# Cross-attention with LayerNorm: a new order of VectorE's prologue, the first query weights on ScalarE's DMA queue, and eight warm-up products

## The chip, the cores and the metric

The kernel runs on one core of one Trainium2 chip. The metric is the device time in microseconds (us) of one execution; a kernel's time is the median of its runs.

## The reference, cut to what matters

Queries `x` (4 batches, 2048 rows, 512 wide) attend to a context of 77 rows for each batch, with 16 heads of 32; a mask marks the context rows that are left out. The result goes through an output projection, is added to `x`, and is normalised by row:

```python
qs = (q @ wq).reshape(Bq, Lq, H, HD).transpose(0, 2, 1, 3)
ks_ = (k @ wk).reshape(Bq, Lk, H, HD).transpose(0, 2, 1, 3)
vs = (v @ wv).reshape(Bq, Lk, H, HD).transpose(0, 2, 1, 3)
scores = jnp.einsum('bhqd,bhkd->bhqk', qs, ks_) / jnp.sqrt(jnp.float32(HD))
scores = jnp.where(mask[:, None, :, :], -jnp.inf, scores)
attn_w = jax.nn.softmax(scores, axis=-1)
attn = jnp.einsum('bhqk,bhkd->bhqd', attn_w, vs)
out = attn @ wo + q
# LayerNorm over the row, times gamma, plus beta
```

All of it is float32.

## The kernel before

The 8192 rows are 64 tiles of 128 (`t`), 32 blocks of two tiles (`b`) and 16 groups of four tiles (`g`). Projections are exact to float32 by splitting: an operand is rounded to a high part (`wqh`, `x0h`, `woh`, `wvh`, `ctx_h`), the rest is a low part (`wql`, `x0l`, ...), and three products (high-high, high-low, low-high) are summed in PSUM. `split` makes the high part on ScalarE and the low part on VectorE.

Nothing is scheduled by a planner: `manual_schedule` is on, so every engine runs its instructions in the order in which the Python code issues them, and an engine that waits for one instruction holds all that stand behind it. Each DMA queue (SyncE's, ScalarE's, GpSimd's) is in order too. PSUM is a ring of eight banks handed out by `bank`.

The work around the change:

- **Prologue** (lines 558 to 631). VectorE clears the tile `warm`, and ten bf16 products on it (`WARM`) keep TensorE busy while the first loads come. SyncE issues the loads: half of `xT0`, `wq` by quarters, the context `ctx_f`, `wk` by quarters, the mask, the other half. For each quarter `c`, `x0` and `wq` are split, and the products of the first query half (`pq_0_m`, m = 0 to 3) are issued; then come the keys (`pk`), the copies out of PSUM, the mask bias of the first tile (`mask_bias`), the value-weight loads (`load_wv`) and `keys_evac`.
- **Main loop**, steps u = 0, 2, 4, ... each for tiles u and u+1. For a tile: `scores` (64 small products into four banks), `maxima` (sixteen VectorE instructions, one per head, which add the mask bias `mb`, write the scores to `pbuf` and reduce their maximum), `exps` (sixteen on ScalarE, with row sums), `recip` (VectorE), `normalise` (GpSimd), `transp` (VectorE's 32x32 transposes of `pbuf` into the block's tile `B`). When both tiles of a block are transposed, `regroup` issues twelve SBUF-to-SBUF DMAs from `B` into `PT` on SyncE's queue. Two steps later `av` multiplies `PT` with the values `vsb` on TensorE (line 397), and `o_proj`, `residual`, `moments`, `scale`, `affine` and `store` follow.
- There are three `pbuf` (tile t uses t mod 3), and the tag `B` has two buffers, which `ctx_f` and `ctx_h` held first.
- **Between them in the first steps**: query products for later groups (`q_visit`) with their copies (`q_evac`, VectorE); the value products (`values`, one for each of batches 0 to 2) with `values_evac` (VectorE); `split_wv` (VectorE, four subtractions); `split_wo` (GpSimd); `mask_nan`, which prepares a column that `moments` reads later; the casts and low parts of the next groups of `x` (`cast_xT` on ScalarE, `split_xT` on GpSimd, line 163).
- In step 2 SyncE's queue holds the load of half a group (`load_xT`, line 154), whose buffer `split_xT` on GpSimd must first have read, and behind it the regroup of block 0.
- From tile 54 on a list written out by hand, `ORDER`, sets the order.

VectorE's order in the first steps of the kernel before:

- step 0: maxima of tile 0 with a query copy, mask bias of the other 15 tiles, `split_wv`, query copy, `recip(0)`, maxima of tile 1, `transp(0)`, `mask_nan`, `recip(1)`;
- step 2: maxima of tile 2 with query copies, `transp(1)`, `values_evac(0)`, query copies, `recip(2)`, maxima of tile 3, `values_evac(1)` and `(2)`, `recip(3)`;
- step 4: maxima of tile 4, `transp(2)`, `transp(3)`, query copies, `recip(4)`, maxima of tile 5.

Of the kernel before, what the change touches and what calls it, by code (L numbers as in the profile page):

```python
# [17 lines left out]
P = 128  # L18
# [13 lines left out]
GRP = 2 * BLK  # L32
MASKED = -3.0e38
EPS = 1.0e-5
WARM = 10
NPB = 3
KSCALE = 1.0 / HD**0.5
LATE = 48
# [29 lines left out]
def xattn_layernorm(  # L68
# [68 lines left out]
    def wview(w, c):  # L137
        return w[c * P : (c + 1) * P, :]

    def split(hi, lo, src):  # L140
        nc.scalar.copy(hi, src)
        nc.vector.tensor_tensor(lo, src, hi.bitcast(F32), ALU.subtract)
# [9 lines left out]
    def load_xT(g, c):  # L152
        fx[g, c] = sb.tile([P, 2, GRP], F32, tag="xtf", name=f"xtf_{g}_{c}")
        nc.sync.dma_start(fx[g, c], xT[g, :, c : c + 2])
# [50 lines left out]
    def keys_evac(pks, m):  # L205
        for i, eng in ((m, nc.scalar), (m + 1, nc.vector)):
            pk = pks[i][:, : NB * (NK + 1)].rearrange("p (b k) -> p b k", b=NB)[:, :, :NK]
            for dst, src in ((kct[:, i, :, TAIL_K:], pk), (kct[:, i, :, :TAIL_K], pk[:, :, NK - TAIL_K :])):
                if eng is nc.scalar:
                    eng.activation(dst, src, AF.Copy, scale=KSCALE)  # L210
                else:
                    eng.tensor_scalar(dst, src, KSCALE, None, ALU.mult)
# [27 lines left out]
    def values_evac(r):  # L240
        pv = vd.pop(r)
        for b, p0, k0, n in ((r, 0, 0, NK2), (NB - 1, NK2, 32 * r, 32)):
            src, dst = (a.rearrange("p (q a d) -> p q a d", a=2, d=HD) for a in (pv[p0 : p0 + n], vsb[k0 : k0 + n, b]))
            rows_of = vm[k0 : k0 + n, :, 0][:, None, :, None].to_broadcast((n, NP, 2, HD))
            nc.vector.tensor_tensor(dst, src, rows_of, ALU.mult)
# [9 lines left out]
    def split_wv():  # L255
        for c in range(NC_D):
            nc.vector.tensor_tensor(wvl[c], stage_b[:, 0, c], wvh[c].bitcast(F32), ALU.subtract)
# [19 lines left out]
    def mask_bias(b, ts=slice(0, TPB)):  # L277
        mb, nz, m8 = bat[b]
        nc.vector.tensor_scalar(mb[:, ts, TAIL_K:], m8[:, ts], MASKED, None, ALU.mult)
        nc.vector.tensor_scalar(mb[:, ts, :TAIL_K], m8[:, ts, NK - TAIL_K :], MASKED, None, ALU.mult)  # L280
# [26 lines left out]
    def maxima(t, lo, hi):  # L307
        pb = pbuf[t % NPB]
        mb = bat[t // TPB][0]
        nm = nmax[t]  # L310
        for h in HEADS[lo:hi]:
            g, j = divmod(h, GH)
            nc.vector.tensor_tensor_reduce(  # L313
                pb[:, h // 2, (h % 2) * NK : (h % 2 + 1) * NK],
                scs[t][j][:, g * NK : (g + 1) * NK],
                mb[:, t % TPB, keys_of(h)],
                -1.0,
                3.0e38,
                ALU.add,
                ALU.min,  # L320
                accum_out=nm[:, h : h + 1],
            )
# [36 lines left out]
    def transp(t):  # L359
        b, tt = divmod(t, 2)  # L360
        if b not in bts:
            bts[b] = sb.tile([P, 5, 2 * NP * 32], F32, tag="B", name=f"B_{b}")
        if b < NBLK - 1:
            bt = bts[b].rearrange("p c (q t r) -> p c q t r", q=NP, t=2)[:, :, :, tt, :]
        else:
            bt = bts[b].rearrange("p c (t q r) -> p c q t r", q=NP, t=2)[:, :, :, tt, :]
        nc.vector.transpose(  # L367
            bt.rearrange("p c q r -> p q c r"),
            pbuf[t % NPB].rearrange("p q (c r) -> p q c r", c=5),
        )  # L370
# [184 lines left out]
        nc.vector.scalar_tensor_tensor(od[t], od[t], mvs[t, 1][:, 2:3], rows.get(1, bet), ALU.mult, ALU.add)  # L555


    nc.vector.memset(warm, 0.0)
    nc.gpsimd.memset(mhalf, -0.5)
    nc.gpsimd.memset(mneg, -1.0)  # L560
    for pb in pbuf:
        nc.gpsimd.memset(pb[:, :, 2 * NK :], 0.0)
    pw = bank("pw")
    for i in range(WARM):
        nc.tensor.matmul(pw, warm[:, :P], warm, start=True, stop=True)

    for c in range(0, NC_D, 2):
        fx[0, c] = sb.tile([P, 2, GRP], F32, tag="xtf", name=f"xtf_0_{c}")
# [3 lines left out]
    f0 = {c: fx[0, c].rearrange("p c r -> p (c r)").rearrange("p (h c r) -> p h c r", h=2, c=2) for c in (0, 2)}  # L572
    for c in range(0, NC_D, 2):
        nc.sync.dma_start(f0[c][:, 0], xT0[0, :, c : c + 2])
        nc.sync.dma_start(stage_a[:, 0, c], wview(wq, c))
        nc.sync.dma_start(stage_a[:, 0, c + 1], wview(wq, c + 1))
    for c in range(0, NC_D, 2):
        nc.sync.dma_start(ctx_f[:, c : c + 2], ctxT[:, c : c + 2])
    for c in range(NC_D):
        nc.sync.dma_start(stage_a[:, 1, c], wview(wk, c))  # L580
    load_mask(0)
    for c in range(0, NC_D, 2):
# [1 line left out]
    value_rows()  # L584
    pq0 = [bank(f"pq_0_{m}") for m in range(NG)]
    for c in range(NC_D):
        split(x0h[:, c], x0l[:, c], f0[c // 2 * 2][:, 0, c % 2])
        split(wqh[:, c], wql[:, c], stage_a[:, 0, c])
        for m in range(NG):
            for n, (w, r) in enumerate(((wqh, x0h), (wqh, x0l), (wql, x0h))):  # L590
                nc.tensor.matmul(
                    pq0[m][:, :BLK],
                    w[:, c, m * P : (m + 1) * P],
                    r[:, c, :],
                    start=(c == 0 and n == 0),
                    stop=(c == NC_D - 1 and n == 2),
                )
# [11 lines left out]
        split(*(a[:, c : c + 2, BLK:] for a in gx[0]), f0[c][:, 1])  # L609
    deal_last()  # L610
    q_visit(0, 0)
    mask_bias(0, slice(0, 1))
    gate(stage_a[:, 1, NC_D - 1, D - 1 :])
    load_wv()
    for m in range(0, NG, 2):
        keys_evac(pks, m)
    for c in range(0, NC_D, 2):
        fx[1, c] = stage_a[:, 0, c : c + 2]
        nc.sync.dma_start(fx[1, c], xT[1, :, c : c + 2])
# [8 lines left out]
    def visits(u):  # L628
        return early[u] if u in early else [divmod(u + 5, 4)] * (u + 5 < 4 * NGRP)

    def pieces(u):
        return casts.get(u) or [((u + 8) // 4, u % 4)] * (u + 8 < 4 * NGRP)

    evac = [(0, 0)]
    for u in range(0, 2 * CUT, 2):
        n = u // 2
        m, k = divmod(u, TPB)

        for q in pieces(u + 2):
            if u >= 4:  # L640
                load_xT(*q)
        for t in (u - 4, u - 3):
            if t >= 0:
                load_x(t)
        scores(u)
        maxima(u, 0, H // 2)
        for q in evac:
            q_evac(*q)
        maxima(u, H // 2, H)
        for q in pieces(u):  # L650
            cast_xT(*q)
        exps(u, 0, H)
        for q in pieces(u):
            split_xT(*q)
        if u == 0:
            mask_bias(0, slice(1, TPB))
            split_wv()
        if u >= 6:
            o_proj(u - 6)
        for v in {2: (0,)}.get(u, ()):  # L660
            values(v)
        for q in visits(u):
            q_visit(*q)
        if u >= 6:
            residual(u - 6)
            moments(u - 6)
        if u == 4:
            transp(2)
        if u == 2:
            load_xT(*pieces(4)[0])  # L670
        if u:
            transp(u - 1)
            regroup(n - 1)
        for v in list(vd):
            values_evac(v)
        if u >= 8:
            scale(u - 8)
            scale(u - 7)
        if u >= 8:
            affine(u - 8)  # L680
        for q in visits(u):
            q_evac(*q)
        if u == 0:
            load_wo()
            nc.gpsimd.memset(ident, 0.0)
            nc.gpsimd.affine_select(ident, ident, [[-1, P]], ALU.not_equal, 1.0, base=0, channel_multiplier=1)
        if k == TPB - 6 and m + 1 < NB:
            load_mask(m + 1)
        if k == TPB - 4 and m + 1 < NB:
            mask_bias(m + 1)  # L690
        if k == TPB - 2 and m + 1 < NB:
            mask_nan(m + 1)

        recip(u)
        if u >= 4:
            av(n - 2)
            av_hi(n - 2, 0)
            av_hi(n - 2, 1)
        scores(u + 1)
        maxima(u + 1, 0, H // 4)  # L700
        if u >= 4:
            av_lo(n - 2, 0)
        maxima(u + 1, H // 4, H // 2)
        if u >= 4:
            av_lo(n - 2, 1)
        maxima(u + 1, H // 2, H)
        normalise(u)
        for c in {0: (0, 1), 2: (2, 3)}.get(u, ()):
            split_wo(c)
        if u >= 8:  # L710
            affine(u - 7)
        exps(u + 1, 0, H // 4)
        exps(u + 1, H // 4, H)
        if u >= 5:
            o_proj(u - 5)
        if u >= 5:
            residual(u - 5)
        if u != 2:
            transp(u)
        for v in {2: (1, 2)}.get(u, ()):  # L720
            values(v)
            values_evac(v)
        evac = visits(u + 1)
        for q in evac:
            q_visit(*q)
        if u >= 5:
            moments(u - 5)
        if u == 0:
            mask_nan(0)
        recip(u + 1)  # L730
        normalise(u + 1)
        if u >= 8:
            store(u - 8)
            store(u - 7)
# [90 lines left out]
```

## Time and profile before

| what | us |
|---|---|
| median of three runs | 518.78 |
| lowest and highest of them | 516.29, 519.95 |
| time of the profiled execution | 517.11 |
| its span, first to last instruction | 515.3 |
| TensorE (PE) busy | 504.5 (98%) |
| VectorE (DVE) busy | 473.8 (92%) |
| ScalarE (ACT) busy | 470.3 (91%) |
| GpSimd (POOL) busy | 418.1 (81%) |

The mean granted clock of TensorE in the profiled execution is 0.996. In the profile's rows L313 is the line that an instruction comes from; `out<-in` are the program's tiles; x12 counts the instructions of a row; square brackets give the idle time of the engine just before the row, and what ended it. In timelines the first two columns are the start and the length in us. Matmuls are pipelined: the pace is told by the distance of their starts, not by their lengths. In a row of windows come the stretch, its length, the busy time of PE, PEld, DVE, ACT and POOL with the number of instructions in brackets, the granted clock, the DMA share and GB/s. SPq is SyncE's DMA queue, DVEq VectorE's queue of waits.

### The profile page before, as it was taken

What the parts mean: (1) busy time and instruction counts of PE and PEld (TensorE: products, weight loads), DVE (VectorE), ACT (ScalarE), POOL (GpSimd) and SP (SyncE); (2) the same over time, 40 slices, a digit from 0 to 9 for tenths busy, and PEclk for the clock granted to TensorE, in tenths of its full rate; (3) what the DMA queues carried; (4) which work ended last, traced back from release to release, by engine and by line L of the source; (5) the groups of instructions that cost most, each with busy time, mean ns of one, the idle gap of its engine ahead of it and who ended that gap; (6) DMA issues with size and microseconds to landing.
All of it is one profiled execution on the core that took longest, in us unless ns stands there. A gap on an engine that the chain in (4) does not pass through costs nothing.

```text
span 515.3 us, 20436 instructions
## 1 busy us (share of the span) xinstructions
PE 504.5 (98%) x6838; PEld 385.7 (75%) x6838; DVE 473.8 (92%) x2572; ACT 470.3 (91%) x2241; POOL 418.1 (81%) x375
## 2 busy tenths in 40 slices
PE   9999989999999999999999999999999999999994
PEld 6987767777777777777777777777777877777672
DVE  5699998899999888989999898889999989999996
ACT  6789999999899999999899999999899999999841
POOL 0658549889799988888889989889889988857996
PEclk9999999999999999999999999999999999999998
DMA  8946678787778878788778878869878887776665
GB/s 304 402 146 161 175 201 206 205 233 207 202 186 229 222 217 226 211 215 223 182 208 235 232 199 213 227 178 240 216 201 220 212 217 232 203 200 176 170 215 209
DMA packets 58936, 110.24 MB, mean 214 GB/s; under 512 B 9392, under 2 KB 11312, under 8 KB 58832
## 3 DMA queue, kind: packets, MB, share of 16 engines
q1 hardware_dynamic: 56144, 103.62, 72.6%
q0 software_dynamic: 2128, 4.85, 3.4%
q8 instruction: 55, 0.90, 0.8%
q10 hardware_dynamic: 560, 0.46, 0.3%
q14 instruction: 49, 0.40, 0.3%
HBM read 41.79 MB, written 16.78 MB: 114 GB/s over the span
## 4 chain that ended last, share of the span: by engine, by line
PE 74%; DVE 8%; POOL 5%; DMA 4%; SPq 3%; ACT 3%; issue 2%; DVEq 0%; POOLq 0%; ACTq 0%
PE po L463 30%; PE pq L170 26%; PE pa L397 9%; PE sc L299 9%; ACT pbuf L327 2%; SPq L379 2%; DVE B L367 2%; DMA PT<-B 2%; DVE pbuf L313 2%; DMA stage_b<-wo 1%; DMA stage_a<-wk 1%; POOL mvt L529 1%; POOL o_end L542 1%; DVE AL L432 1%; POOL o_end L493 1%
## 5 line engine op out<-in xcount | busy, mean ns | idle before, releaser
L327 ACT ACTIVATE pbuf<-pbuf,nm 128x77 f32<-128x77 f32 x1024 | 352.4, 349 | 17.3 <-DVE nm L313 15.8
L327 ACT ACTIVATION_READ_ACCUMULATOR pbuf<-pbuf,nm 128x1 f32 x1024 | 194.0, 189 | 0.0
L313 DVE CUSTOM_DVE_ANT_0 pbuf<-sc,mb 128x77 f32<-128x77 f32 x1024 | 170.5, 230 | 22.3 <-PE sc L299 22.2
L343 POOL TENSOR_TENSOR pbuf<-pbuf,ri 128x1232 f32<-128x1232 f32 x63 | 142.2, 2258 | 23.5 <-DVE ri L338 19.4
L170 PE MATMUL pq<-xth,wqh 128*128 128x512 f32 (+1 forms) x256 | 98.8, 386 | 0.0
L170 PE MATMUL pq<-xtl,wqh 128*128 128x512 f32 (+1 forms) x256 | 97.9, 382 | 0.0
L170 PE MATMUL pq<-xth,wql 128*128 128x512 f32 (+1 forms) x256 | 97.9, 382 | 0.0
L367 DVE STREAM_TRANSPOSE B<-pbuf 128x1280 f32<-128x1280 f32 x64 | 95.5, 1493 | 2.2 <-DMA PT<-B 1.7
L463 PE MATMUL po<-woh,AH 128*128 128x512 f32 x232 | 96.8, 417 | 0.0
L463 PE MATMUL po<-wol,AH 128*128 128x512 f32 x232 | 90.7, 391 | 0.0
L463 PE MATMUL po<-woh,AL 128*128 128x512 f32 x232 | 88.8, 391 | 0.0
L313 DVE DVE_READ_ACCUMULATOR2_ANT nm<- 128x1 f32 x1024 | 83.9, 82 | 0.0
L493 POOL TENSOR_TENSOR o<-o,gam 128x512 f32<-128x512 f32 x50 | 65.6, 1312 | 14.4 <-ACT o L489 14.3
L299 PEld LDWEIGHTS sc<-kct,q 32*64 32x64 f32 x4096 | 51.4, 130 | 24.2 <-issue 23.5
L494 POOL TENSOR_TENSOR o<-o,bet 128x512 f32<-128x512 f32 x50 | 64.5, 1289 | 3.9
L163 POOL TENSOR_TENSOR xtl<-xtf,xth 128x1024 fp32r<-128x1024 f32 x28 | 67.0, 2394 | 0.0
L299 PE MATMUL sc<-kct,q 32*64 32x77 f32 x4096 | 61.5, 237 | 0.3 <-DVE nm L313 0.3
L397 PE MATMUL pa<-PT,vsb 96*32 96x256 f32 x960 | 58.0, 382 | 1.9 <-DVE st L471 1.3
L170 PEld LDWEIGHTS pq<-xth,wqh 128*128 128x128 f32 x256 | 48.1, 188 | 9.8
L170 PEld LDWEIGHTS pq<-xth,wql 128*128 128x128 f32 x256 | 48.1, 188 | 9.4
L170 PEld LDWEIGHTS pq<-xtl,wqh 128*128 128x128 f32 x256 | 48.1, 188 | 9.1
L463 PEld LDWEIGHTS po<-woh,AH 128*128 128x128 f32 x232 | 43.5, 187 | 12.5 <-issue 0.7
(139 smaller groups left out, 700.5 us busy)
## 6 DMA issues: line engine op xcount, KB each, us to landing
PT<-B SPq DMA_DIRECT2D x352, 128.0 KB
xtf<-xT SPq DMA_DIRECT2D x28, 512.0 KB
o<-x SPq DMA_DIRECT2D x56, 256.0 KB
out<-o SPq DMA_DIRECT2D x56, 256.0 KB
PT<-B POOLq DMA_DIRECT2D x20, 128.0 KB, 4.0
o_end<-x SPq DMA_DIRECT2D x8, 256.0 KB
out<-o_end SPq DMA_DIRECT2D x8, 256.0 KB
xtf<-xT SPq DMA_DIRECT2D x4, 256.0 KB
```

The lines of the kernel that those rows point to most:

```text
L163: nc.gpsimd.tensor_tensor(l, fx.pop((g, c)), h.bitcast(F32), ALU.subtract)
L170: nc.tensor.matmul(pq, w[:, c, m * P : (m + 1) * P], r[:, c, rs], start=(n == 0), stop=(n == 11))
L299: nc.tensor.matmul(sc[j][half : half + P // 2, g * NK : (g + 1) * NK], qs[q, g, r0 : r0 + P // 2], kct[q, g, t // TPB, keys_of(j)], start= ...
L313: nc.vector.tensor_tensor_reduce(pb[:, h // 2, (h % 2) * NK : (h % 2 + 1) * NK], scs[t][j][:, g * NK : (g + 1) * NK], mb[:, t % TPB, keys_ ...
L327: nc.scalar.activation(pb[:, h // 2, (h % 2) * NK : (h % 2 + 1) * NK], pb[:, h // 2, (h % 2) * NK : (h % 2 + 1) * NK], AF.Exp, bias=nmax[t ...
L343: nc.gpsimd.tensor_tensor(pv, pv, rv.to_broadcast((P, NP, 2, NK)), ALU.mult)
L367: nc.vector.transpose(bt.rearrange("p c q r -> p q c r"), pbuf[t % NPB].rearrange("p q (c r) -> p q c r", c=5),)
L379: queue.dma_start(pts[b][32 * c : 32 * c + 32, i, :, cols], src)
L397: nc.tensor.matmul(pas[b, g // 2][HD * j : HD * (j + 1), (g % 2) * BLK : (g % 2 + 1) * BLK], vsb[:, 2 * b // TPB, HD * h : HD * (h + 1)], ...
L463: nc.tensor.matmul(pos[t], a[:, c, rs], w[:, c, :], start=(first and n == 0), stop=(n == 11))
L493: nc.gpsimd.tensor_tensor(o, o, gam, ALU.mult)
L494: nc.gpsimd.tensor_tensor(o, o, bet, ALU.add)
```

## The change

VectorE's order in the first steps becomes:

- prologue: VectorE itself copies the high part of `wq`'s first quarter; the mask bias of eight tiles instead of one; `mask_nan` right after the keys' copies;
- step 0: maxima of tile 0 with a query copy, mask bias of the other eight tiles, query copy, maxima of tile 1, `split_wv`, `recip(0)`;
- step 2: half of tile 2's maxima, `recip(1)`, query copies, the other half, `transp(0)`, `values_evac(0)`, `transp(1)`, `recip(2)`, maxima of tile 3, query copies, `values_evac(1)`, `recip(3)`, `transp(2)`;
- step 4: maxima of tile 4, `transp(3)`, `values_evac(2)`, query copies, `recip(4)`, maxima of tile 5.

GpSimd clears the warm-up tile (a quarter of the old width, read four times by each product), and there are eight products. The first quarter of `wq` is issued on ScalarE's queue; half of the context is issued behind the first two quarters of `wk`. The first query products are ordered by operand pair, then by `m`. GpSimd's order of the large operations, TensorE's order from the keys on, and everything from step 6 on stay.

```diff
-WARM = 10
+WARM = 8
@@
-    nc.vector.memset(warm, 0.0)
+    nc.gpsimd.memset(ident[:, : P // 2], 0.0)
@@
-        nc.tensor.matmul(pw, warm[:, :P], warm, start=True, stop=True)
+        nc.tensor.matmul(pw, warm[:, :P], warm[:, None, :P].to_broadcast((P, 4, P)), start=True, stop=True)
@@
-        nc.sync.dma_start(stage_a[:, 0, c], wview(wq, c))
+        (nc.sync if c else nc.scalar).dma_start(stage_a[:, 0, c], wview(wq, c))
         nc.sync.dma_start(stage_a[:, 0, c + 1], wview(wq, c + 1))
-    for c in range(0, NC_D, 2):
-        nc.sync.dma_start(ctx_f[:, c : c + 2], ctxT[:, c : c + 2])
     for c in range(NC_D):
+        if c % 2 == 0:
+            nc.sync.dma_start(ctx_f[:, c : c + 2], ctxT[:, c : c + 2])
         nc.sync.dma_start(stage_a[:, 1, c], wview(wk, c))
@@
     for c in range(NC_D):
+        if c == 0:
+            nc.vector.tensor_copy(wqh[:, 0], stage_a[:, 0, 0])
         split(x0h[:, c], x0l[:, c], f0[c // 2 * 2][:, 0, c % 2])
-        split(wqh[:, c], wql[:, c], stage_a[:, 0, c])
-        for m in range(NG):
-            for n, (w, r) in enumerate(((wqh, x0h), (wqh, x0l), (wql, x0h))):
+        if c == 0:
+            nc.vector.tensor_tensor(wql[:, 0], stage_a[:, 0, 0], wqh[:, 0].bitcast(F32), ALU.subtract)
+        else:
+            split(wqh[:, c], wql[:, c], stage_a[:, 0, c])
+        for n, (w, r) in enumerate(((wqh, x0h), (wqh, x0l), (wql, x0h))):
+            for m in range(NG):
@@
-    mask_bias(0, slice(0, 1))
+    mask_bias(0, slice(0, TPB // 2))
@@
         keys_evac(pks, m)
+    mask_nan(0)
@@ main loop, first half of a step
         maxima(u, 0, H // 2)
+        if u == 2:
+            recip(1)
+            normalise(1)
@@
         if u == 0:
-            mask_bias(0, slice(1, TPB))
-            split_wv()
+            mask_bias(0, slice(TPB // 2, TPB))
@@
-        if u == 4:
-            transp(2)
         if u == 2:
             load_xT(*pieces(4)[0])
+        if u == 2:
+            transp(0)
+            values_evac(0)
         if u:
             transp(u - 1)
             regroup(n - 1)
-        for v in list(vd):
-            values_evac(v)
+        if u == 4:
+            values_evac(2)
@@
-        for q in visits(u):
-            q_evac(*q)
+        if u != 2:
+            for q in visits(u):
+                q_evac(*q)
@@ second half
-        recip(u)
+        if u:
+            recip(u)
@@
         maxima(u + 1, H // 2, H)
+        if u == 0:
+            split_wv()
+            recip(0)
+        if u == 2:
+            for q in visits(u):
+                q_evac(*q)
         normalise(u)
@@
-        if u != 2:
+        if u >= 4:
             transp(u)
-        for v in {2: (1, 2)}.get(u, ()):
-            values(v)
-            values_evac(v)
+        if u == 2:
+            values(1)
+            values_evac(1)
+            values(2)
@@
-        if u == 0:
-            mask_nan(0)
-        recip(u + 1)
-        normalise(u + 1)
+        if u:
+            recip(u + 1)
+            normalise(u + 1)
+        if u == 2:
+            transp(2)
```

## The prediction

> **What bounds the kernel now.** I read the chain of waits on the page first, then the same chain in order of time, then each engine's timeline over the first 70 us, since the change touches nothing that runs later.
>
> ```profile
> PE 74%; DVE 8%; POOL 5%; DMA 4%; SPq 3%; ACT 3%; issue 2%; DVEq 0%; POOLq 0%; ACTq 0%
> ```
> TensorE sets the end. In order of time (start, length, what):
>
> ```profile
> 49.88 2.69 DMA PT<-B
> ...
> 68.22 1.93 PE pa L397 x32
> 70.15 0.88 PE sc L299 x54
> ...
> 434.29 0.89 PE sc L299 x54
> 435.18 0.22 DVE pbuf L313
> ```
> From 68.22 to 435.18 us every piece of the chain is TensorE; what follows hangs on the scores at 434.29. So whatever moves the `av` of block 1 at 68.22 moves the end one for one. Before 68.22 the chain runs through the regroup transfers, and TensorE's timeline shows where they hold it:
>
> ```profile
> 41.44 0.95 PE L299 MATMUL sc<-kct,q 32*64 32x77 f32 x64
> ...
> 57.32 0.50 PE L170 MATMUL pq<-xth,wqh 128*128 128x512 f32 x1
> ...
> 60.28 0.95 PE L299 MATMUL sc<-kct,q 32*64 32x77 f32 x64
> ...
> 66.53 0.39 PE L170 MATMUL pq<-xth,wql 128*128 128x512 f32 x1
> 68.22 1.93 PE L397 MATMUL pa<-PT,vsb 96*32 96x256 f32 x32 [1.30 <-DVE st L471]
> ```
> The last query matmul starts at 66.53 and would be followed after 0.25 us (twelve from 57.32 to 60.28), so TensorE is at `av` by 66.78 and loses 1.44 there. VectorE is named as the releaser, but the program makes this matmul wait for the twelve transfers of block 1's regroup. SyncE's timeline shows their issue:
>
> ```profile
> 41.19 0.33 SPq L154 DMA_DIRECT2D xtf<-xT  x1
> 41.62 8.86 SPq L379 DMA_DIRECT2D PT<-B  x12
> ...
> 56.17 9.22 SPq L379 DMA_DIRECT2D PT<-B  x12
> ```
> Block 0's last transfer lands by the chain at 52.57 (49.88 + 2.69). Block 1's issues end at 65.39; with the same 2.69 they land at 68.1. So 68.22 is fixed by when the second transpose of block 1 ends.
>
> **The change, part by part.** The part that decides is the transpose of tile 2 (`transp(2)`). It moves from the middle of step 4, behind all of tile 4's maxima, to the end of step 2, ahead of them. In both programs it waits for all twelve transfers of block 0's regroup, because block 1's `B` takes the buffer that these transfers read. VectorE works in order, so all that stands behind it waits too. Before, on VectorE:
>
> ```profile
> 46.71 2.81 DVE L245 TENSOR_TENSOR vsb<-pv,small 96x512 f32<-96x512 f32 x4
> 50.14 0.25 DVE L338 RECIPROCAL ri<-sum 128x16 f32<-128x16 f32 x1 [0.62 <-ACT pbuf L327]
> ...
> 53.23 2.90 DVE L367 STREAM_TRANSPOSE B<-pbuf 128x1280 f32<-128x1280 f32 x2 [0.19 <-issue]
> 56.06 1.25 DVE L187 COPY q<-pq 128x512 f32<-128x512 f32 x2
> ```
> and, in the view of line 367, the waits of VectorE's queue (least, median and longest in ns, first and last start):
>
> ```profile
> L367 DVEq EVENT_SEMAPHORE  x8: 49/50/749, 52.1 to 74.4; - x8
> ```
> The first of those waits began at 52.1; if it is the one of 749 ns, the transfers were in by 52.85, just when tile 4's maxima ended. The old order hid the wait behind these maxima. The new one has no such cover. Tile 3's maxima began at 44.2 (46.71 less 2.53, the price of sixteen worked out below) and its last reciprocal at 50.14; they now begin at 41.9 or 42 (41.44, less a start gain of 0.4, plus 0.95), so the reciprocal comes at about 47.8 and `transp(2)` is next. VectorE idles some 5 us.
>
> When do those transfers land now? SyncE's load at 41.19 stands ahead of them and waits for GpSimd:
>
> ```profile
> 30.54 2.26 POOL L343 TENSOR_TENSOR pbuf<-pbuf,ri 128x1232 f32<-128x1232 f32 x1 [4.41 <-DVE ri L338]
> 32.76 2.55 POOL L267 TENSOR_TENSOR wol<-stage_b,woh 128x512 fp32r<-128x512 f32 x2
> 36.54 2.26 POOL L343 TENSOR_TENSOR pbuf<-pbuf,ri 128x1232 f32<-128x1232 f32 x1 [1.24 <-DVE ri L338]
> 38.77 4.74 POOL L163 TENSOR_TENSOR xtl<-xtf,xth 128x1024 fp32r<-128x1024 f32 x2
> ```
> GpSimd's order stays; the first step starts when tile 0's reciprocal is done. That one is put behind tile 1's maxima and the split of the value weights. The rows that price this:
>
> ```profile
> 18.01 0.62 DVE L212 TENSOR_SCALAR kct<-pk 128x308 f32<-128x308 f32 x2 [0.95 <-PE pk L196]
> ...
> 22.59 0.24 DVE L313 CUSTOM_DVE_ANT_0 pbuf<-sc,mb 128x77 f32<-128x77 f32 x1 [3.07 <-PE sc L299]
> ...
> 25.72 1.35 DVE L279 TENSOR_SCALAR mb<-m 128x1155 bf16<-128x1155 uint8 x1
> ...
> 27.21 1.28 DVE L257 TENSOR_TENSOR wvlAH<-stage_b,wvh 128x512 fp32r<-128x512 f32 x2
> ...
> 29.61 0.68 DVE L189 COPY q<-pq 128x512 f32<-128x512 f32 x1
> 30.21 0.24 DVE L338 RECIPROCAL ri<-sum 128x16 f32<-128x16 f32 x1
> ...
> 34.28 1.39 DVE L284 TENSOR_REDUCE nz<-m 128x16 f32<-128x1232 uint8 x1
> ```
> A copy takes 0.60 (29.61 to 30.21), so sixteen maxima take 2.53 (22.59 to 25.72 less one copy). From 25.72 on: half of the mask rows instead of fifteen sixteenths, 0.9 instead of 1.49; the copy 0.6; tile 1's maxima 2.5; the split 2.4 (27.21 to 29.61). The reciprocal then starts at 32.1 against 30.21, 1.9 later. GpSimd however no longer stops 1.24 us for tile 1's reciprocal, since tile 1's maxima start at 27.2 instead of 30.4. Net: load and regroup start 0.6 later, less the start gain.
>
> **The start gain.** Query weights 0 go out on ScalarE's queue, VectorE makes their high part itself, the order of products asks first for what is ready first, and key weights 0 are issued ahead of half the context. ScalarE and TensorE before:
>
> ```profile
> 4.27 0.62 ACT L141 CAST wqh<-stage_a 128x512 fp32r<-128x512 f32 x1 [0.43 <-DMA stage_a<-wq]
> ```
> ```profile
> 1.18 4.45 PE L565 MATMUL pw<-ident 128*128 128x512 bf16 x10 [1.18 <-DVE ident L558]
> 5.07 0.78 PE L591 MATMUL pq<-xth,wqh 128*128 128x256 f32 x1
> ...
> 6.06 0.28 PE L591 MATMUL pq<-xth,wqh 128*128 128x256 f32 x1
> ...
> 11.44 0.31 PE L196 MATMUL pk<-ctx_h,woh 128*128 128x312 f32 x1
> ...
> 11.85 0.41 PE L196 MATMUL pk<-ctx_h,wol 128*128 128x312 f32 x1
> ...
> 18.69 0.28 PE L170 MATMUL pq<-xth,wqh 128*128 128x256 f32 x1
> ```
> From 5.07 to 6.06 only three products start; the other 45 take 5.38, 0.12 each. VectorE's copy from SBUF is not in the trace; its bounds are the cast of the same shape on ScalarE, 0.62, and nothing. The weights landed at 4.27. The first real matmul then starts between 4.3 and 5.07; I take 4.7, in the middle. At the early pace that is two or three more products by 6.06, 0.3. At the key products the third one starts 0.41 after the first, where two steps at the later pace ((18.69 - 11.85) / 46 = 0.15) are 0.30; earlier key weights save that 0.1. Gain 0.4, bounds 0 and 0.9 (4.3, and the wait gone). The two warm-ups dropped end the series at about 4.5, ahead of the operands, and cost nothing unless the clock rises later.
>
> Beside that, the Trainium skill's page DMA: Bandwidth & Descriptors, section "Issuing engines are not separate DMA queues", says that a second issuing engine saves only sequencer time. By it the weights would come little before 4.27, and the gain would be nearer to 0.2 and the sum 0.2 more. No row of before has two engines issuing loads at the start.
>
> **At nothing.** `mask_nan` (1.39 and two small ones) moves into the 3.07 us in which VectorE sat idle ahead of 22.59, and the larger first mask piece into the 0.95 ahead of 18.01; without that cover they would add some 1.8 and 0.6. The products keep their number, and from step 6 on the order is the old one.
>
> **The sum.** Block 0's regroup lands at 52.85 + 0.6 - 0.4 = 53.05; `transp(2)` starts at 53.15. Behind it, one after the other: transpose 1.42 (53.23 to 56.06 by two), tile 4's maxima 2.53, transpose of tile 3 1.42. Block 1's regroup can start at 58.52, and the old one started when the transposes ended, at 56.13: 2.4 later, which puts block 1's `av` at 70.6. TensorE gets there on another path: the fourth score buffer of tile 5 now comes from the last value product, whose evacuation (2.81 by two, 1.40) follows that transpose, so it is free at 59.9; the scores end at 60.8, 3.5 after 57.32; 66.78 + 3.5 = 70.3. The transfers decide. **The sum is 2.4 us slower.** Against the profiled execution (span 515.3, time 517.11) this is 519.5; the median shown is 1.67 above that execution, and on it the time is 521.2. With the chain's landing of 52.57 and the gain of 0.9 it is 1.6, with a gain of 0 it is 2.8: 520.4 to 521.6.
>
> **The rivals.**
>
> *The clock falls in the new gap.* Block 0's `av` ends by 56.1 (its second half waits for the first four of tile 4's maxima, 53.15 + 1.42 + 0.63, and takes 0.93). From then to 59.9 TensorE does 3 of 64 score products. What idleness does, in the windows at the end of the trace (the column ahead of the last two is the granted clock):
>
> ```profile
> 508.30:511.20 2.90, 0.00 (x0) 0.00 (x0) 1.90 (x4) 0.00 (x0) 2.39 (x5) 1.00 0.41 160
> 511.20:515.30 4.10, 0.00 (x0) 0.00 (x0) 1.06 (x2) 0.00 (x0) 0.00 (x0) 0.50 0.37 142
> ```
> After 2.9 us without a matmul the granted clock was 0.50. The new gap is 3.8. At the start it took from 1.18 to 6.06 until the pace doubled, 4.9 us; at half pace that costs 2.4 at most, and nothing if the clock holds. With 2 of it, less the 0.3 that TensorE has in hand on the transfers: 2.4 + 1.7 = 4.1, 522.9. Against it: the three products, and the 1.44 us at 66.78 that did no harm. The Trainium skill, TensorE: Matmul & The Clock Gate, Part 1, says that a free-running window of about 3.4 us sets the clock; by it the same gap would cost it in one run and not in the next.
>
> *The transfers are in early and the start gain reaches the end (faster).* With block 0's regroup landed before 47.8, `transp(2)` does not wait, the 1.44 close, and 0.4 comes on top: 516.9. It is no loss from a landing of 50.6 on (53.05 less 2.4). Against it: GpSimd's steps from the reciprocal at 31.7 on (0.33 to its start, then 2.22, 2.54, 2.23, 2.4 by their rows) end at 41.4, and the transfers then took 11 us.
>
> *No net effect.* The landing comes at about 50.6: 518.8. For it only that the twelve issues may be quicker than 8.86.
>
> *VectorE's lateness stays.* Tile 5's maxima start at 60.9 instead of 57.4; if later steps never make it good, TensorE follows by 3.5: 522.3. Against it: the chain after 68.22 shows no wait on VectorE, so there is slack to make it good.
>
> **How the numbers follow.** Stall alone 0.47; stall and clock 0.33; VectorE's lateness 0.08; no net effect 0.08; faster 0.04. One per cent, 5.2 us, is about what a measurement of this kernel can tell from no change: below 513.6 is faster, above 524.0 slower. The runs of before lie from 516.29 to 519.95, so each case carries some 1.2 us of its own. Slower: a third of the clock case and a little of the next: 0.14. Faster: 0.03, since even the full gain is 2 us. Within: 0.83. The range goes from the case of no net effect less part of its scatter, 518.0, to the clock case plus its own, 524.2.
>
> **What would show it.** After the change: VectorE idle some 5 us ahead of one transpose that starts near 53; TensorE waiting until about 59.9 inside tile 5's scores; block 1's `av` at about 70.6, and no new TensorE wait after 75. A granted clock below 1.00 near 60 means the second case. First query matmul at 4.3 to 5.0, key products at 11.0 to 11.4. The prediction is wrong if the transpose of tile 2 starts before 51, or if `av` of block 1 starts before 68.2.

## The result, and the profile after

The changed kernel takes 525.94 us (median of 4 runs, 524.50 to 527.31) against 518.68 of the kernel before beside it (516.29 to 519.95): a ratio of 1.0155, 95% interval 1.0121 to 1.0188. The forecast of 521.2 had the sign, but not the size: 7.3 us were lost where its sum said 2.4. Measured again among the experiments (11), the changed kernel took 523.26, 1.0115 (1.0086 to 1.0143): 5.7 us lost, still more than twice the sum. The profiled execution of the changed kernel took 524.5.

Its page, head and granted clock in 40 slices (the fifth digit from the left covers 52 to 65 us; before, only the last slice read below 9):

```profile
span 522.7 us, 20426 instructions
...
PEclk9999899999999999999999999999999999999998
```

TensorE's timeline, without the query and output products that lie between these rows (start, length, what, and the idle time before it with its releaser):

```profile
21.13 0.95 PE L299 MATMUL sc<-kct,q 32*64 32x77 f32 x64
...
56.06 1.07 PE L397 MATMUL pa<-PT,vsb 96*32 96x256 f32 x16 [0.60 <-PE pq L170]
58.34 1.07 PE L397 MATMUL pa<-PT,vsb 96*32 96x256 f32 x16 [1.22 <-DVE nm L313]
59.34 0.58 PE L299 MATMUL sc<-kct,q 32*64 32x77 f32 x4
60.24 0.41 PE L299 MATMUL sc<-kct,q 32*64 32x77 f32 x2 [0.32 <-DVE nm L313]
62.86 1.37 PE L299 MATMUL sc<-kct,q 32*64 32x77 f32 x58 [2.20 <-DVE vsb L245]
...
75.03 1.93 PE L397 MATMUL pa<-PT,vsb 96*32 96x256 f32 x32
```

The last row answers to the 68.22 of before: block 1's `av` is 6.81 later, though tile 0's scores start 0.52 earlier (21.13; before 21.65). From `av` to the end of the span it is 447.7 (before 447.1). So nearly all of the loss lies between the first scores and this `av`. I call that the stretch: 46.57 before, 53.90 after, 7.33 more. It leaves out the start, and all experiments below are read by it. It is coarse: the changed kernel profiled twice (here and in 11) gave 53.90 and 52.82, so differences below about 1 us between two single profiles are not resolved.

VectorE, SyncE and the chain of waits in order of time, from the changed kernel:

```profile
18.91 1.43 DVE L284 TENSOR_REDUCE nz<-m 128x16 f32<-128x1232 uint8 x1
20.37 2.34 DVE L285 TENSOR_SCALAR nz<-nz 128x16 f32<-128x16 f32 x1
22.75 2.33 DVE L286 TENSOR_SCALAR nz<-nz 128x16 f32<-128x16 f32 x1
24.99 0.23 DVE L313 CUSTOM_DVE_ANT_0 pbuf<-sc,mb 128x77 f32<-128x77 f32 x1
...
34.20 0.23 DVE L338 RECIPROCAL ri<-sum 128x16 f32<-128x16 f32 x1
...
55.93 1.51 DVE L367 STREAM_TRANSPOSE B<-pbuf 128x1280 f32<-128x1280 f32 x1 [5.67 <-DMA PT<-B]
...
60.02 1.50 DVE L367 STREAM_TRANSPOSE B<-pbuf 128x1280 f32<-128x1280 f32 x1
61.45 1.36 DVE L245 TENSOR_TENSOR vsb<-pv,small 96x512 f32<-96x512 f32 x2
```
```profile
43.89 0.33 SPq L154 DMA_DIRECT2D xtf<-xT  x1
44.31 8.47 SPq L379 DMA_DIRECT2D PT<-B  x12
```
```profile
52.18 3.57 DMA PT<-B
...
64.22 4.31 PE pq L170 x12
```

Two things are to be seen. First, the wait that the prediction put ahead of the transpose of tile 2 is there (5.67; "some 5"), but the transpose starts at 55.93 and not at 53.15: everything ahead of it comes 2.5 to 2.8 later than the prediction had it, back to tile 0's maxima at 24.99 (22.59 in the kernel before, less the start gain of 0.4). Ahead of these stand the two scalings of `mask_nan`, 128x16 numbers each, which take 2.34 and 2.33 us. The same two before, on VectorE:

```profile
35.70 0.17 DVE L285 TENSOR_SCALAR nz<-nz 128x16 f32<-128x16 f32 x1
35.91 0.17 DVE L286 TENSOR_SCALAR nz<-nz 128x16 f32<-128x16 f32 x1
```

Second, the twelve query products behind tile 5's scores take 4.31, where twelve such products took 2.96 in the kernel before (57.32 to 60.28). The windows say why (PE busy is the first number behind the length; the granted clock stands third from the end):

```profile
60.30:67.20 6.90, 4.70 (x67) 3.73 (x68) 6.82 (x29) 6.65 (x36) 2.25 (x1) 0.51 0.58 132
67.20:70.00 2.80, 2.80 (x73) 2.11 (x73) 2.30 (x13) 2.80 (x17) 0.00 (x0) 1.00 0.89 207
```

For 6.8 us TensorE ran at half clock, with about 4.3 us of work in it: the prediction's first rival.

### The profile page after: what moved, and what is told of

Same layout as the page of the kernel before. It is cut to its first block, busy times and chain, and to the rows that moved or that the text cites. A ratio compares the mean times of both kernels' runs of the same rounds, so it can differ in the third digit from the quotient of the medians.

```text
span 522.7 us, 20426 instructions
## 1 busy us (share of the span) xinstructions
PE 507.6 (97%) x6836; PEld 387.5 (74%) x6836; DVE 477.6 (91%) x2572; ACT 470.0 (90%) x2240; POOL 418.2 (80%) x376
## 4 chain that ended last, share of the span: by engine, by line
PE 79%; DVE 6%; POOL 4%; ACT 4%; DMA 3%; SPq 1%; issue 1%; DVEq 0%; POOLq 0%
PE po L463 31%; PE pq L170 27%; PE sc L299 10%; PE pa L397 9%; ACT pbuf L327 3%; DMA PT<-B 2%; DVE B L367 2%; DVE pbuf L313 1%; SPq L379 1%; PE pk L196 1%; PE pq L596 1%; POOL mvt L529 1%; POOL o_end L542 1%; DMA xtf<-xT 1%; DMA o<-x 1%
## 5 line engine op out<-in xcount | busy, mean ns | idle before, releaser
L299 PEld LDWEIGHTS sc<-kct,q 32*64 32x64 f32 x4096 | 52.8, 131 | 28.5 <-issue 25.0
L299 PE MATMUL sc<-kct,q 32*64 32x77 f32 x4096 | 63.8, 239 | 3.9 <-DVE vsb L245 2.2
```

The lines of the kernel that those rows point to most:

```text
L299: nc.tensor.matmul(sc[j][half : half + P // 2, g * NK : (g + 1) * NK], qs[q, g, r0 : r0 + P // 2], kct[q, g, t // TPB, keys_of(j)], start= ...
```

## The experiments

In the table a kernel's stretch comes from its profiled execution. Times are medians, ratios are against the kernel before run beside it (its median was 518.68 beside the changed kernel, and 517.3 to 517.7 beside the others). 12 and 15 are one kernel (1.0034 and 1.0066), and so are the changed kernel and 11 (1.0155 and 1.0115): so far do two measurements of one thing lie apart here.

| | edit | time | ratio (95%) | stretch |
|---|---|---|---|---|
| | the kernel before | 518.68 | 1 | 46.57 |
| | the changed kernel | 525.94 | 1.0155 (1.0121 to 1.0188) | 53.90 |
| 11 | the changed kernel, again | 523.26 | 1.0115 (1.0086 to 1.0143) | 52.82 |
| 1 | scalings late | 522.41 | 1.0120 (1.0073 to 1.0166) | 52.19 |
| 10 | `mask_nan` ahead of the keys | 522.42 | 1.0092 (1.0061 to 1.0123) | 51.85 |
| 13 | warm-up of ten | 523.81 | 1.0116 (1.0084 to 1.0147) | 51.94 |
| 5 | filled | 523.02 | 1.0098 (1.0062 to 1.0133) | 51.25 |
| 6 | scalings late, filled | 521.14 | 1.0075 (1.0045 to 1.0105) | 50.10 |
| 7 | evacuation 2 ahead | 523.03 | 1.0084 (1.0040 to 1.0127) | 50.64 |
| 9 | scalings late, evacuation 2 ahead | 521.05 | 1.0060 (1.0041 to 1.0080) | 48.75 |
| 12 | as 9, filled | 519.64 | 1.0034 (1.0008 to 1.0059) | 49.42 |
| 15 | as 12, again | 521.38 | 1.0066 (1.0038 to 1.0093) | 48.86 |
| 14 | as 12, but scalings as in the change | 522.91 | 1.0105 (1.0062 to 1.0148) | 50.05 |
| 2 | transpose of tile 2 back | 518.25 | 1.0016 (0.9994 to 1.0037) | 48.13 |
| 3 | both undone | 517.58 | 1.0002 (0.9974 to 1.0030) | 45.53 |
| 4 | kernel before, `mask_nan` early | 517.90 | 1.0035 (1.0003 to 1.0067) | 48.24 |
| 8 | candidate | 516.99 | 1.0003 (0.9983 to 1.0024) | 45.54 |

### Undoing one part at a time (1 to 4)

1, on the changed kernel (`nan_scale` is the two scalings alone; `mask_nan` keeps the reduction):

```diff
         if u == 0:
             mask_bias(0, slice(TPB // 2, TPB))
+            nan_scale(0)
```

> The changed kernel, but with the two scalings of mask_nan (128x16) behind the second piece of the mask rows, where GpSimd is idle, not beside its two splits at 20.3 to 25.05. Theory held scalings: each was held until GpSimd's split ended (2.34 and 2.33 against 0.17), and this 4.3 us is why the prediction missed. Then the scalings take 0.17 again, the first maxima start at about 22.1 instead of 24.99, the transpose of tile 2 at about 53.1 instead of 55.93, and the time is that of the prediction's sum, 521.2 where the clock holds, 523 where TensorE still falls to half clock in its gap. Rival, place of the transpose and clock alone: the lateness of the first maxima is absorbed in the later wait for the transfers, and the time stays at 525 to 526.

2, on the changed kernel:

```diff
+        if u == 4:
+            transp(2)
         if u:
             transp(u - 1)
             regroup(n - 1)
-        if u == 4:
-            values_evac(2)
...
             values(2)
+            values_evac(2)
...
-        if u == 2:
-            transp(2)
```

> The changed kernel, but with the transpose of tile 2 and the evacuation of value product 2 in their places of before (the scalings stay beside GpSimd's splits). Theory held scalings: the first maxima stay at 25.0, the transfers of block 0 land at about 55.8, but tile 4's maxima run ahead of that wait; the transposes end about 58.8 against 56.13, block 1's av starts at about 70.9, TensorE's gap is spread and small, the granted clock is 1.00, and the time is 521 to 522. Rival, the place of the transpose explains everything: the time is that of before, 518 to 519.

3 is both edits together.

> The changed kernel with both undone: scalings where GpSimd is idle, transpose of tile 2 and evacuation 2 in their places of before. What is left is the start (first weights on ScalarE's queue, warm-up of eight, order of products), the larger first mask piece, and the reciprocal of tile 0 behind tile 1's maxima. Theory held scalings plus the moved wait: 518.2 to 518.8, block 1's av at 67.7 to 68.3, clock 1.00 to the tail. Rival, something else in the start or the reciprocal's place costs time too: 520 or more.

4, on the kernel before:

```diff
         keys_evac(pks, m)
+    mask_nan(0)
...
-        if u == 0:
-            mask_nan(0)
```

> The kernel before, with mask_nan alone moved to behind the keys' evacuation, as the change has it. Theory held scalings: each scaling takes about 2.3 us beside GpSimd's splits at 20.0 to 24.8, the first maxima start at about 25.2 instead of 22.59, load and regroup of block 0 some 2.4 later, block 1's av at about 70.3, the time 520.5 to 521.5. Rival, the idle ahead of the maxima hides it as the prediction said: first maxima at 22.6, time 518 to 519.

With both undone the loss is gone: ratio 1.0002, and TensorE reaches block 1's `av` at 67.03 with no wait there. TensorE and VectorE of experiment 3:

```profile
54.39 1.93 PE L402 MATMUL pa<-PT,vsb 96*32 96x256 f32 x32
56.26 0.95 PE L304 MATMUL sc<-kct,q 32*64 32x77 f32 x64
57.41 0.50 PE L170 MATMUL pq<-xth,wqh 128*128 128x512 f32 x1 [0.20 <-DVE q L187]
...
67.03 1.93 PE L402 MATMUL pa<-PT,vsb 96*32 96x256 f32 x32
```
```profile
53.87 2.90 DVE L372 STREAM_TRANSPOSE B<-pbuf 128x1280 f32<-128x1280 f32 x2 [1.59 <-DMA PT<-B]
```

So the start and the later reciprocal of tile 0 cost nothing that can be measured. The moved transpose, with the evacuation that the change put behind it (1 against 3), costs 5 to 6 us (4.8 by the medians, 1.2% by the ratios), most of the loss, and this is clear of the noise. The scalings alone, in the order of before, were held as expected; VectorE of experiment 4:

```profile
21.03 1.55 DVE L285 TENSOR_SCALAR nz<-nz 128x16 f32<-128x16 f32 x1
22.62 2.32 DVE L286 TENSOR_SCALAR nz<-nz 128x16 f32<-128x16 f32 x1
```

In that profile the stretch grows by 1.67, and the time is 517.90 (1.0035), where 520.5 to 521.5 was expected. In experiment 2 the held scalings do not show above the noise (1.0016), where 521 to 522 was expected: my theory had their price too high there, although the stretch of its one profile is 2.6 longer than that of 3. The trace of experiment 1 is as the theory had it: the lateness is gone (the transpose at 53.45), and the clock fell all the same. Its time, 522.41, lies near the 523 expected for that case. But the times do not show that it is faster than the changed kernel: its ratio is 1.0120, against 1.0155 and, measured again, 1.0115.

### The clock (5, 6)

Extra products of the warm-up's form ahead of tile 5's scores, nine of them in 5 and twelve in 6, into a bank that the scores then overwrite:

```diff
         sc = scs[t] = [bank(f"sc_{t}_{j}") for j in range(GH)]
+        for _ in range(9 * (t == 5)):
+            nc.tensor.matmul(sc[0], warm[:, :P], warm[:, None, :P].to_broadcast((P, 4, P)), start=True, stop=True)
```

> The changed kernel with nine extra matmuls of the warm-up's form (128x512 bf16, about 0.21 each at full clock) ahead of tile 5's scores, into the first of their banks, which the scores then overwrite. They stand where TensorE only waits (59.3 to 62.86). Theory clock: the half clock from 60.3 to 67.2 (4.3 us of TensorE's work in it, so 2.1 lost) comes from the idle before it; with the fill it is gone or half as long, and the time falls by 1 to 2 us to 524 to 525. Rival, the clock loses nothing on the path (only the wait counts): unchanged at 525.9, or later by what the fill adds.

> The variant with the scalings late (522.4), with twelve of the same extra matmuls at the same place, 56.9 to 59.4, in a wait that lasts to 60.4. Theory clock: half clock from 59.0 to 65.9 had 5.5 us of TensorE's work in it, 2.7 lost; filled, the granted clock stays 1.00 and the time falls to 519.5 to 520.5, which is the prediction's sum without the clock. Rival: unchanged, 522 or more.

More work for TensorE shortened the stretch of both: 6 against 1, from 52.19 to 50.10; 5 against the changed kernel, from 53.90 (52.82 in 11) to 51.25. The times point the same way (1.0075 against 1.0120, 1.0098 against 1.0155 and 1.0115), but their intervals overlap, and 6 came out at 521.14 where 519.5 to 520.5 was expected. TensorE of experiment 6 and its windows:

```profile
57.29 2.76 PE L300 MATMUL sc<-ident 128*128 128x512 bf16 x12
...
60.80 0.90 PE L306 MATMUL sc<-kct,q 32*64 32x77 f32 x58 [0.46 <-DVE vsb L245]
...
71.14 1.93 PE L404 MATMUL pa<-PT,vsb 96*32 96x256 f32 x32
```
```profile
56.00:63.00 7.00, 6.25 (x98) 3.69 (x99) 6.92 (x41) 6.76 (x37) 0.51 (x1) 1.00 0.30 70
```

The granted clock stays 1.00, and the 58 scores take 0.90 where they took 1.37. All seven profiles with the moved transpose and no fill show the fall, and none of the five with a fill does. For the other executions only the mean clock is on record: of the 36 without a fill 31 read 0.992 or less, the rest 0.993 or 0.994, which single executions of the kernel before read too; the 31 with a fill read 0.994 to 0.998. The fall costs 1.8 to 2.1 of the stretch (experiments 1, 10 and 13 against 6); by the changed kernel and 11 against 5 it is 2.7 and 1.6.

### What stands behind the wait (7, 9, 12)

7, on the changed kernel; 9 is the same on experiment 1; 12 is 9 with six extra products as above:

```diff
         if u == 2:
+            values_evac(2)
             transp(2)
...
-        if u == 4:
-            values_evac(2)
```

> The changed kernel with the evacuation of value product 2 ahead of the transpose of tile 2 (VectorE idles there), not behind the transpose of tile 3. Tile 5's fourth score bank is then free when tile 4's maxima are done, about 60.0, and not at 62.8. Theory: TensorE's wait at these scores shrinks by 2.6, and block 1's av is then set by the regroup's transfers (issue from about 60.1 with two pieces less work ahead, landing about 72): 72 against 75.0, time 523. Rival, the transfers and VectorE's lateness set the time anyway: 525.5 or more.

> Two edits on the changed kernel: the scalings late (where GpSimd is idle) and the evacuation of value product 2 ahead of the transpose of tile 2. What stays of the change's price is that transpose's own wait for the transfers. Theory: transpose of tile 2 at about 53.3, tile 5's scores done about 58.3, block 1's av at 71.2 to 71.6, half clock in one stretch near 58 to 65; 520 to 521.5. In the seventh experiment's profile the scalings happened not to be held (they started 0.3 ahead of GpSimd's split), so if holding is what spread its times from 520.0 to 524.3, these times lie closer, near its lower end. Rival, the spread has another source: 523 again, with the same spread.

> The ninth experiment's kernel with six extra matmuls of the warm-up's form ahead of tile 5's scores (into the first of their banks, overwritten), in waits of some 1.2 us together. Theory clock: the granted clock stays 1.00, 518.5 to 519.5, some 2 us less than without. Rival, the clock falls by the waits that are left (at the query products and at av): as without, 520 to 521.5.

Only the order on VectorE changes: the evacuation that frees tile 5's fourth score bank no longer stands behind the wait. TensorE of experiment 9, where the wait of 2.20 is gone:

```profile
56.68 0.89 PE L304 MATMUL sc<-kct,q 32*64 32x77 f32 x58 [0.32 <-DVE nm L318]
58.59 0.50 PE L170 MATMUL pq<-xth,wqh 128*128 128x512 f32 x1 [1.02 <-DVE q L187]
...
69.69 1.93 PE L402 MATMUL pa<-PT,vsb 96*32 96x256 f32 x32
```
The clock still fell (mean 0.991 to 0.994), but filling it (12, and 15) did not shorten the stretch further: 48.75 without, 49.42 and 48.86 with; my expected 2 us did not come.

In 12 and 15, where the clock holds, TensorE waits at block 1's `av`, 0.54 and 0.23. The profile names VectorE's maxima of tile 6, from which this `av` takes nothing; it starts 1.91 behind the end of the regroup's issues in both (70.16 and 67.75), so I take this for the wait for the transfers. In 9 there is no such wait. Its issues end at 66.70; by the same distance, which is an estimate, its transfers land at about 68.6, and `av` starts at 69.69. So the half clock still costs up to 1.1 there. That 12 and 15 are no shorter fits with later transfers: the transpose of tile 2 starts at 53.16 in 15 and at 52.37 in 9, although the issues of block 0 end together (50.43 and 50.45). So once TensorE is early enough and the clock holds, the transfers of block 1 seem to decide; this is argued from these rows, and why transfers land later in one execution than in another is open.

What is left against the kernel before, 2.2 to 2.9, I put down to the wait of the transpose itself. The times of 9 spread as widely (518.56 to 522.96) as those of 7 (519.97 to 524.26), so the hold of the scalings is not what spreads them, as I had expected. 15 came out at 521.38 where 519 to 520 was expected; in its profile the part behind `av` took 452.0, longer than in any other, and why is open.

### Why a scaling of 16 columns takes 2.3 us (10, 11, 13, 14)

10, on the changed kernel:

```diff
     load_wv()
+    mask_nan(0)
     for m in range(0, NG, 2):
         keys_evac(pks, m)
-    mask_nan(0)
```

> The changed kernel with mask_nan ahead of the keys' evacuation, not behind it: VectorE idles there and the scalings end at about 17.8, 2.5 before GpSimd's split starts. Theory, whichever of the two engines starts first keeps the other out: the scalings take 0.17 each, the first maxima start at about 22.3, the time is that of the first experiment, 522 to 523. Rival, it is the scalings themselves that are slow after a reduction: still 2.3 each, 525 to 526.

> The changed kernel as it is, beside the others on one chip. Theory: its scalings start within 0.3 us of GpSimd's split, so they are held in some executions and free in others; times near 522 (free) and near 524.5 (held), each up to 2 more by the phase of the clock at the start. Rival: held always, 524.5 and more.

13 is the changed kernel with `WARM = 10`:

> The changed kernel with a warm-up of ten again. In the profiles so far the granted clock rose late (at 9.0 to 9.9) in 4 of 11 executions with eight, which leave 0.4 to 0.9 of pause ahead of the first product, and in none of 3 with ten, which leave none; a late rise moves the first scores from about 21.0 to 22.8. Theory, the pause lets the clock rise late: some 0.5 to 0.8 less on the median than the changed kernel, 522.5 to 525, and a rise by 8.0 in the profile. Rival, the phase is chance and not the pause: no difference, 523.3 to 525.9.

> The twelfth experiment's kernel (evacuation 2 ahead, six extra matmuls, clock held at 1.00) with the scalings back where the change has them, behind the keys' evacuation. Theory held scalings: where they are held, the first maxima start 2.3 to 2.9 later, and the time is 1 to 2.5 above that of the twelfth's kernel, run beside it. Rival, the lateness is taken up by the wait of the transpose: no difference, 519.6.

> The twelfth experiment's kernel again, as the partner of the fourteenth: scalings late, evacuation 2 ahead, filled. 519 to 520 by both theories; granted clock 1.00 to the tail.

Ahead of the keys, where GpSimd is idle, the scalings take 0.17 each and the stretch falls to 51.85. VectorE of experiment 10:

```profile
17.35 0.17 DVE L285 TENSOR_SCALAR nz<-nz 128x16 f32<-128x16 f32 x1
17.56 0.17 DVE L286 TENSOR_SCALAR nz<-nz 128x16 f32<-128x16 f32 x1
```

The place in the order is not what decides, but which engine starts first. GpSimd's subtraction in the changed kernel's profile starts 0.07 ahead of the first scaling (20.37):

```profile
20.30 4.75 POOL L163 TENSOR_TENSOR xtl<-stage_a,xth 128x1024 fp32r<-128x1024 f32 x2 [5.42 <-DMA stage_a<-xT]
```

In the profile of experiment 13, which differs in two warm-up products alone, it starts 0.16 behind the second scaling, and both go free. VectorE, then GpSimd:

```profile
20.26 0.17 DVE L285 TENSOR_SCALAR nz<-nz 128x16 f32<-128x16 f32 x1
20.47 0.17 DVE L286 TENSOR_SCALAR nz<-nz 128x16 f32<-128x16 f32 x1
```
```profile
20.63 4.73 POOL L163 TENSOR_TENSOR xtl<-stage_a,xth 128x1024 fp32r<-128x1024 f32 x2 [5.28 <-ACT xth L159]
```

The stretches of these two executions, 53.90 and 51.94, price the hold at 2.0 in the changed order. Other pairs of profiles give less: 11 against 13 0.9, 5 against 6 1.2, and 14 against 12 and 15, with the clock held, 0.6 and 1.2. So its price in the changed order is 0.6 to 2.0. In the times it barely shows: 14 is 1.0105 against 1.0066 for 15 run beside it, with intervals that overlap, and 4 is 1.0035 with an interval that just leaves out 1. The warm-up of ten gained nothing that the times show (1.0116; the changed kernel again 1.0115). Experiment 11 did not show the free executions that I expected: its profile was held (1.55 and 2.32), and its times lie from 522.2 to 525.5. How often the hold strikes is not shown by the times, only that it did in 6 of the 8 profiles with the scalings behind the keys' evacuation.

### A version that might beat both (8)

Experiment 3 with the reciprocal of tile 0 ahead of tile 1's maxima and ten warm-up products:

```diff
-        if u:
-            recip(u)
+        recip(u)
...
             split_wv()
-            recip(0)
```

> Both undone as in the third experiment, and the reciprocal of tile 0 ahead of tile 1's maxima again (behind the smaller mask piece), warm-up of ten. Theory: GpSimd's first step starts at about 28.5 instead of 30.54, load and regroup of block 0 at about 39 instead of 41.2, the transpose of tile 2 does not wait, TensorE waits nowhere between 28 and 68, block 1's av at 66.8 to 67.2 against 68.22: 516 to 517, 1 to 1.5 us faster than before. Rival, VectorE's work and not the transfers sets that stretch: no gain over the third experiment, 517.3.

No gain: 1.0003, stretch 45.54 against 45.53 of experiment 3. GpSimd's first step did start at 28.77, but its next one waited 1.24 for a weight load, and in the stretch TensorE had nothing left to win: at block 1's `av` it waited 0.20 in all, in experiment 3 not at all.

## Why the prediction failed, point by point

Two steps failed. The term `mask_nan`, put at nothing, was held beside GpSimd and cost 0.6 to 2.0 us of the stretch. And the forecast took the case in which the clock holds, where the half clock cost about 2.

- **What bounds the kernel, and the place of the loss: right.** `av` of block 1 carried 6.81 of the 7.4 by which the span grew, and no new wait of TensorE above 0.3 came behind it.
- **The wait of the transpose of tile 2: right in kind.** VectorE idled 5.67 ahead of it. In the filled experiment 6, where neither the clock nor the scalings disturb, block 1's `av` comes 2.92 later than before, against 2.1 to 2.4 in the sum. The transpose started at 53.88 there instead of 53.15, and the work behind it to the evacuation took 5.51 (to 59.39) instead of 5.37.
- **"The transfers decide": wrong for the changed kernel.** TensorE's own path through tile 5's scores came later: 1.37 of scores and 4.31 of products follow the 62.86 at which the last bank is free. Of the profiles with the moved transpose, only 12 and 15 show a wait of TensorE at block 1's `av`: there the evacuation stands ahead and the clock holds (0.54 and 0.23).
- **"At nothing": the first step that failed.** The prediction hid `mask_nan` in 3.07 us of VectorE's idle time and added up its lengths, 1.39 and two small ones. It looked at the engine's own idle time and not at what GpSimd does then. The row of the same instruction in block 1 of the kernel before would have told it; VectorE, then GpSimd:

```profile
249.38 1.42 DVE L284 TENSOR_REDUCE nz<-m 128x16 f32<-128x1232 uint8 x1
250.83 1.28 DVE L285 TENSOR_SCALAR nz<-nz 128x16 f32<-128x16 f32 x1
252.15 0.17 DVE L286 TENSOR_SCALAR nz<-nz 128x16 f32<-128x16 f32 x1
```
```profile
249.45 1.27 POOL L493 TENSOR_TENSOR o<-o,gam 128x512 f32<-128x512 f32 x1 [0.54 <-ACT o L489]
250.80 1.29 POOL L494 TENSOR_TENSOR o<-o,bet 128x512 f32<-128x512 f32 x1
```

  The scaling that starts 0.03 behind GpSimd's instruction lasts until that one ends (252.09); the reduction beside the other ran its usual 1.42. The Trainium skill, SBUF — State Buffer, section "Who interferes with whom", has the rule: VectorE and GpSimd share one pair of ports, a `tensor_scalar` can enter a mode that needs it, whoever issues first has it for the whole instruction, and `tensor_reduce` never contends on trn2. The rows agree: 2.34 behind the subtraction, 0.17 ahead of it.
- **The clock: the second step that failed, and the rival that came true.** It had 0.33 against 0.47, on the ground that three score products stood in the gap and that 1.44 us of idleness had done no harm. Its price of 4.1 in all was near what came without the hold: `av` at 72.96 in experiment 13, 4.74 later than before. The prediction also drew from the Trainium skill (TensorE: Matmul & The Clock Gate, Part 1) that a free-running window would make the gap cost something in one run and not in the next; here it fell in all seven profiles with the gap, for 6.8 us in six of them and for 3.4 in that of experiment 9, and by their mean clock in most of the other executions. No profile here showed the gap without the fall.
- **The start: right.** First query matmul 5.00, key products 11.14, first scores 0.52 earlier.

The parts in the stretch, as differences along the chain before, 12 or 15, 6, 13, changed kernel: wait of the transpose 2.3 to 2.9, evacuation behind it 0.7 to 1.2, half clock 1.8, hold 2.0. They add up to the 7.33 by construction, so the sum is no check on them; how firm each is shows in the other pairs above, which give 1.6 to 2.7 for the half clock and 0.6 to 1.2 for the hold. Less 0.52 of the start and plus 0.6 behind `av` (not settled; it varied between 447.0 and 448.6 in all profiles but that of 15) this is the 7.4 of the span. Of the 4.9 that the forecast missed, about 2 are the clock and 0.6 to 2.0 the hold; the rest is the size of the wait, the end, and the scatter by which the second measurement lost only 5.7.

## What to carry to other kernels

Idle time of an engine is cover for a moved instruction only if no other engine holds what it needs then: look for the same instruction elsewhere in the trace and compare its least with its greatest length, and see what ran beside it. When an instruction that waits is moved ahead of others in an in-order queue, list all that is now behind it; the evacuation that freed a PSUM bank turned VectorE's wait into TensorE's gap. And a gap of TensorE is to be priced with the half clock behind it, unless a later wait would hold TensorE as long anyway.

## What the runs showed of the hardware

The pace of the first products doubles at a time that differs from execution to execution: their starts lie 0.21 us apart, then 0.12. From 4.8 to 9.4 us experiment 2's profile did 20 matmuls and experiment 13's 36:

```profile
4.80:9.40 4.60, 4.32 (x20) 4.35 (x21) 4.18 (x10) 3.48 (x8) 0.00 (x0) 1.00 1.01 370
```
```profile
4.80:9.40 4.60, 4.39 (x36) 4.22 (x36) 4.06 (x10) 3.39 (x9) 0.00 (x0) 1.00 1.03 367
```

Their first scores start at 22.87 and 21.02; over all profiles from 20.80 to 22.97. The late doubling came in 5 of the 13 profiles with eight warm-up products and in none of the four with ten, too few to tell the pause ahead of the first product from chance. How much of the scatter of the times comes from it was not measured. The column of the granted clock reads 1.00 in both, so this has to be read from the counts. That is why the parts are read from the stretch, and not from the span.
